# Five early attention heads by another softmax path, and the last batch's feed-forward part in two halves of its tokens

## The chip, the cores and the metric

The kernel runs on one core of one Trainium2 chip. Its time is the device time of one execution in microseconds (us), as the median of several runs of the same program. One further execution was recorded by the hardware profiler; the profile and the trace are those of that execution, and their times count from the start of its span. The engines are called TensorE (PE in the profile, with PEld for its weight loads), VectorE (DVE), ScalarE (ACT), GpSimd (POOL) and SyncE (SP, which issues most of the transfers).

## What is computed

The input `x` holds 16 batches of 512 tokens of 128 numbers. Each batch goes through one attention block and one feed-forward block (FFN), each with a layernorm in front, one behind, and a residual addition:

```
x = x + layernorm(attention(layernorm(x)))
x = x + layernorm(ffn(layernorm(x)))

attention: q, v = projections of x, 16 heads of 8 numbers
  bucket[s,h] = 6 sign bits of (q[s,h], 1) @ hyperplanes
  scores      = q q^T / sqrt(128)
  attn        = softmax(scores * (62 + [bucket equal]))       512 x 512 a head
  out         = attn @ v

ffn: h = silu(x W1^T * s1) * (x W2^T * s2)                    128 -> 512
     h = gelu(h H1^T * sh1);  h = gelu(h H2^T * sh2)          512 -> 512, twice
     y = h W3^T * s3                                          512 -> 128
```

The matrix of scores is symmetric: the queries stand in for the keys. All is float32, but for the score products, which are made of three bfloat16 parts of q, and the coefficients 62 and 63.

## The kernel before, in words

The tokens of a batch are four tiles (t = 0 to 3) of 128. There are 16 x 16 = 256 heads, numbered j through all batches, in groups of four.

**The order of the work is written by a planner.** The class `Order` (lines 47 to 187) is a small simulator that runs while the program is built. Each piece of work is a Python generator that yields steps: an engine, a planned cost in us, a rank and a function that emits the instructions. The planner keeps a clock for each engine, takes the ready step of lowest rank (ties by the order of offering), and emits it. ScalarE's choice also counts the time at which the step became ready, and 4 us for a change of activation table. `Pool` objects hold the names of buffers; `get` and `put` take and return them. On the chip each engine then runs its instructions in exactly this order, and waits where data isn't there.

**One head** takes this way:
1. `gather` (788) reads the head's q parts and bucket numbers from DRAM into `ql`, `qr`, `bb`.
2. `scores` (838): TensorE multiplies, one 128x512 tile a t, into one of three PSUM banks (`sp`).
3. `coeffs` (855): VectorE compares buckets and gives 62 or 63 (`co`, four buffers).
4. `logits` (879): VectorE multiplies the two into a logits tile `l` and writes each row's maximum to a column of `mxpad` (line 894). There are 11 buffers for `l` (`LB`); a head keeps its buffer until its group is through the av matmuls.
5. `maxima` (919): for a pair of heads (the first four heads go singly) VectorE transposes the maxima, SP writes them to DRAM (`md`, 928) and reads them back to all partitions (`mb`, 940, three buffers). Since the matrix is symmetric, the maximum of row s is also that of column s, and the weights come out turned, as the av matmul needs them.
6. `softmax` (933): GpSimd subtracts `mb` from the whole head, 128x2048 in one instruction (947); ScalarE takes the exponent in place (952).
7. `attend` (957): when four heads are done, TensorE multiplies them with v (`av`, 973; a column of ones in v gives the sums for the division), ScalarE copies, TensorE turns the result back (`op`, 994), VectorE divides.

**After the four groups of a batch** `residual` (1018) normalizes the output, adds x, normalizes again and turns the result (`tp_f`); `ffn` (1041) does the gates `w` (1088), two layers `hp` (1122), each with a ScalarE activation in pairs of 512 columns, and the last product `yp` (1156); then a last layernorm (`moments`, `rescale`), an addition (1180) and the output (1186). The FFN's matmuls have the lowest rank on TensorE; FFN b begins when FFN b-1 has finished its first hidden layer. `moments` (385) ends in a power -1/2 on GpSimd (450), of one column for each tile.

**At the start** there is little for TensorE, and `activity` (1244) fills it with matmuls of zeros until the first FFN begins. `weights` loads and scales the FFN's weights; `inputs` (510) makes the first layernorm's statistics of later batches on ScalarE.

Of the kernel before, what the change touches and what calls it, by code (L numbers as in the profile page):

```python
# [16 lines left out]
ALU = mybir.AluOpType  # L17
# [173 lines left out]
def tile_lsh_attention_ffn(  # L191
# [43 lines left out]
    LB = 11  # L235
    SLOTS = H * NT
# [130 lines left out]
    mb_bufs = Pool("mb", 3)  # L367
    h_bufs = Pool("h", 3)
# [16 lines left out]
    def moments(src, name, rank, copy=None):  # L385


        q = name[0]
        rs = p2.tile([P, NT], F32, tag=f"rs{q}", name=f"rs_{name}")
        nm = p2.tile([P, NT], F32, tag=f"nm{q}", name=f"nm_{name}")  # L390
        if copy is not None:

            sums = p2.tile([P, 2, NT], F32, tag=f"su{q}", name=f"su_{name}")
# [22 lines left out]
            yield act(1.0, -2, lambda: sum_((0, 1)))  # L416
            yield act(1.0, -2, lambda: sum_((2, 3)))
            src = copy[0]
            copy[1]()
            yield act(1.2, -2, lambda: square((0, 1)))  # L420
            od.loose()
            yield act(1.2, -2, lambda: square((2, 3)))
            mean, var = sums[:, 0, :], sums[:, 1, :]
            factor, sign = float(E) ** -3, -1.0 / E
        else:
            st = p2.tile([P, NT, nc.vector.BN_STATS_DIM], F32, tag=f"st{q}", name=f"st_{name}")
# [5 lines left out]
            def aggr():  # L432
                for t in range(NT):
                    nc.vector.bn_aggr(mv[:, t, :], st[:, t, :])

            yield dve(0.46, rank, lambda: stats((0, 1)))
            od.loose()
            yield dve(0.46, rank, lambda: stats((2, 3)))
            mv = p2.tile([P, NT, nc.vector.BN_AGGR_DIM], F32, tag=f"mv{q}", name=f"mv_{name}")
            yield dve(0.7, rank, aggr)  # L440
            mean, var, sign, factor = mv[:, :, 0], mv[:, :, 1], -1.0, 1.0
        ve = p2.tile([P, NT], F32, tag=f"ve{q}", name=f"ve_{name}")
# [4 lines left out]
                ve, var, AF.Identity, bias=eps if factor == 1.0 else eps3, scale=factor  # L447
            ),
        )
        yield pool(1.0, 0, lambda: nc.gpsimd.tensor_tensor(rs, ve, mhalf[:, 0], op=ALU.pow))  # L450

        def negate():

            for t in range(NT):
                nc.vector.tensor_scalar(
                    nm[:, t : t + 1],
                    mean[:, t : t + 1],
                    sign,
                    rs[:, t : t + 1],
                    op0=ALU.mult,  # L460
                    op1=ALU.mult,
                )

        yield dve(0.28, rank, negate)
        return nm, rs

    def rescale(src, dst, scales):

        nm, rs = scales

        def emit(ts_):
            for t in ts_:
                nc.scalar.activation(
                    dst(t),
                    src[:, t, :],
                    AF.Identity,
                    bias=nm[:, t : t + 1],
                    scale=rs[:, t : t + 1],
                )

        yield act(0.88, -2, lambda: emit((0, 1)))
        yield act(0.88, -2, lambda: emit((2, 3)))

    def turned(xn, xnt_tag, name, k, tp):


        def turn():
            for t in range(NT):
                nc.tensor.transpose(tp[:, ts(t, P)], xn[:, t, :], ident)

        yield pe(0.5, 2, turn)
        xnt = p1.tile([P, S], F32, tag=xnt_tag, name=f"xnt_{name}")
        yield act(0.5, -2, lambda: nc.scalar.copy(xnt, tp))
        od.put(banks, k)
        return xnt

    def norm_transposed(src, xnt_tag, name, rank):

        xn = p2.tile([P, NT, E], F32, tag=f"xn{name[0]}", name=f"xn_{name}", bufs=1)
        scales = yield from moments(src, name, rank)  # L500
        yield from rescale(src, lambda t: xn[:, t, :], scales)
        k = yield get(banks)
        return (yield from turned(xn, xnt_tag, name, k, bank(k, f"tp_{name}")))
# [78 lines left out]
    def prep(b):  # L582
# [14 lines left out]
        if b:  # L597
            yield wait(known[b])
            xn = p2.tile([P, NT, E], F32, tag="xna", name=f"xn_a{b}", bufs=1)
            yield from rescale(xt, lambda t: xn[:, t, :], (nm_x[:, b], rs_x[:, b]))  # L600
            k = yield get(banks)
            xnt = yield from turned(xn, "xnta", f"a{b}", k, bank(k, f"tp_a{b}"))
        else:
            xnt = yield from norm_transposed(xt, "xnta", f"a{b}", 1)
# [274 lines left out]
    def logits():  # L879
        for j in range(B * H):  # L880
            kl = yield get(logit_bufs)
            if j < SINGLES or j % MH == 0:
                km, pair = (yield get(mx_bufs)), []
                mx = mxpads[int(km[2:])]
            l = p1.tile([P, NT, S], F32, tag=kl, name=f"l_{j}")
            base = len(pair) * NT
            for t in range(NT):
# [5 lines left out]
                def emit(t=t + base, sp=sp, co=co, l=l[:, t, :], mx=mx):  # L893
# [17 lines left out]
            ls[j] = (l, kl)  # L911
            pair.append((j, l))
            if j < SINGLES or len(pair) == MH:
                od.spawn(maxima(pair, mx, km))
# [39 lines left out]

    o_tiles = {}

    def attend(gg):
# [24 lines left out]
        for k in range(GH):  # L982
            od.put(logit_bufs, ls.pop(gg * GH + k)[1])
# [34 lines left out]
    def residual(b):  # L1018
# [10 lines left out]
        scales = yield from moments(o, f"o{b}", 1)  # L1029
        kb = yield get(banks)  # L1030
        ybt = bank(kb, f"yb_{b}").rearrange("p (t e) -> p t e", t=NT)
        yield from rescale(o, lambda t: ybt[:, t, :], scales)
        k1 = yield get(x1_bufs)
        x1 = p1.tile([P, NT, E], F32, tag=k1, name=f"x1_{b}")
        yield dve(0.6, 1, lambda: nc.vector.tensor_tensor(x1, ybt, xt, op=ALU.add))
        od.put(banks, kb)
        kx = yield get(xnt_bufs)
        xnt = yield from norm_transposed(x1, kx, f"f{b}", 1)
        od.spawn(ffn(b, x1, k1, xnt, kx))

    def ffn(b, x1, k1, xnt, kx):
# [4 lines left out]
        kh = yield get(h_bufs)  # L1046
        h = p1.tile([P, NC, S], F32, tag=kh, name=f"h_{b}_0")
        there = events(NC)

        def product(w2, c, half, held, h=h, there=there):  # L1050
            yield wait(half)
            kb, g2 = w2
            a, ka = held[c % 2]
            yield dve(
                0.66,
                1,
                lambda: nc.vector.tensor_tensor(h[:, c, :], g2, a, op=ALU.mult),  # L1057
            )
            od.put(ffn_banks, kb)
# [3 lines left out]
        def silus(c0, gates, half, held):  # L1063
            for _ in gates:
                held.append((yield get(a_bufs)))
            tiles = [
                p1.tile([P, S], F32, tag=ka, name=f"a_{b}_{c0 + i}")
# [3 lines left out]
            def emit():  # L1071
                for i, (a, (_, gp)) in enumerate(zip(tiles, gates)):
# [3 lines left out]
            yield act(1.2, 0, emit, "silu")  # L1076
            for kb, _ in gates:
                od.put(ffn_banks, kb)
            held[:] = zip(tiles, list(held))
            od.set(half)  # L1080

        def gate(which, c):
            kb = yield get(ffn_banks)
            gp = bank(kb, f"{which}_{b}_{c}")
            yield pe(
                0.86,
                4,
                lambda: nc.tensor.matmul(  # L1088
                    gp, lhsT=w_sb[which][:, 0, ts(c, P)], rhs=xnt, start=True, stop=True
                ),  # L1090
            )
            return kb, gp

        for c0 in range(0, NC, 2):
            gates = []
            for c in (c0, c0 + 1):
                gates.append((yield from gate("w1", c)))
            half, held = Event(), []
            od.spawn(silus(c0, gates, half, held))
            for c in (c0, c0 + 1):  # L1100
                w2 = yield from gate("w2", c)
                od.spawn(product(w2, c, half, held))
        od.put(xnt_bufs, kx)
        od.set(stages[b][0])

        for layer in (1, 2):
            w = w_sb[f"h{layer}"]
            hin, khin, before = h, kh, there
            kh = yield get(h_bufs)
            h = p1.tile([P, NC, S], F32, tag=kh, name=f"h_{b}_{layer}")  # L1110
            there = events(NC)
            for c0 in range(0, NC, 2):
                got = []
                for c in (c0, c0 + 1):
                    kb = yield get(ffn_banks)
                    hp = bank(kb, f"hp_{b}_{layer}_{c}")
                    for i in range(NC):
                        yield wait(before[i])
                        yield pe(
                            0.86,  # L1120
# [4 lines left out]
                                rhs=hin[:, i, :],  # L1125
# [4 lines left out]
                    got.append((c, kb, hp))  # L1130

                def gelus(got=got, h=h, there=there, sc=w_sb[f"h{layer}s"]):
                    def emit():
                        for c, _, hp in got:
                            nc.scalar.activation(  # L1135
                                h[:, c, :], hp, AF.Gelu, scale=sc[:, c : c + 1]
                            )

                    yield act(1.2, 0, emit, "gelu")
                    for c, kb, _ in got:  # L1140
                        od.put(ffn_banks, kb)
                        od.set(there[c])

                od.spawn(gelus())
            od.put(h_bufs, khin)
            od.set(stages[b][layer])
# [4 lines left out]
        yp = bank(kb, f"yp_{b}")  # L1151
        for t in range(NT):
# [12 lines left out]
        od.put(h_bufs, kh)  # L1165
        od.set(stages[b][3])


        y = p2.tile([P, NT, E], F32, tag="y", name=f"y_{b}", bufs=1)
# [3 lines left out]
            1,  # L1173
            (y, lambda: od.put(ffn_banks, kb)),
        )
        kn = yield get(banks)
        ybt = bank(kn, f"yn_{b}").rearrange("p (t e) -> p t e", t=NT)
        yield from rescale(y, lambda t: ybt[:, t, :], scales)
        z = y
        yield dve(0.6, 1, lambda: nc.vector.tensor_tensor(z, ybt, x1, op=ALU.add))  # L1180
        od.put(banks, kn)
        od.put(x1_bufs, k1)
# [3 lines left out]
            lambda: nc.sync.dma_start(out=out[b].rearrange("(p t) e -> p t e", t=NT), in_=z),  # L1186
# [134 lines left out]
```

## Time and profile before

| what | value |
|---|---|
| median of 3 runs | 1375.74 us (1370.01 to 1375.81) |
| the profiled execution | 1373.08 us |
| its span in the trace | 1371.3 us |
| mean granted TensorE clock | 0.991 |
| busy: PE, DVE, ACT, POOL | 1317.3, 1236.0, 1127.8, 1217.1 us |
| GpSimd's subtractions (947) | 256 of 4552 ns, 1156.1 us |
| logits (894) | 1024 of 681 ns; a new one can start every 0.60 us |
| coefficients (865) | 1024 of 472 ns; one every 0.39 us |
| exponents (952) | 256 of 1907 ns |
| FFN matmuls of 512 columns (1122, 1088) | one each 0.43 us |
| activation tables loaded before lines 952 and 1135 | 86 and 58, of 1283 ns |

How to read it: a row of the profile names the line, the engine, the operation, the tiles (out<-in), how often it ran, and its mean duration. Instructions of one engine overlap a little, so the distance from one start to the next can be shorter than a duration. The durations of matmuls are modelled; the distance from start to start is the safer figure. The 40 digits of an engine are tenths of busy time in 40 equal slices of the span. The granted clock is TensorE's, 1.00 at full speed. "Idle before" tells how long an engine waited ahead of an instruction, and for whom.

### The profile page before, as it was taken

To read this page: it belongs to the slowest core of one execution; us is meant where nothing else is said; L and a number is where in the kernel's file an instruction comes from. 1 tells how busy PE (TensorE), PEld (TensorE's weight loads), DVE (VectorE), ACT (ScalarE), POOL (GpSimd) and SP (SyncE) were. 2 spreads that over 40 slices of the span, in tenths; PEclk is the share of its full clock that TensorE was granted. 3 is DMA by queue.
4 is the path that set the end of the run, shared out by engine and by line. 5 is a ranking of instruction groups with operands and counts; after the bars stand their busy time and mean duration, and the time that the engine had idled before them with its cause. 6 is when DMAs were issued, how large, how long until landed. Compare 5 with 4: busy or idle time off the path is not lost.

```text
span 1371.3 us, 21177 instructions
## 1 busy us (share of the span) xinstructions
PE 1317.3 (96%) x5922; PEld 550.9 (40%) x5922; DVE 1236.0 (90%) x3989; ACT 1127.8 (82%) x1607; POOL 1217.1 (89%) x319
## 2 busy tenths in 40 slices
PE   9999999999889999999999999999999999999996
PEld 3433334334334434343434434343434434343443
DVE  5999999999889999999999999999999999998210
ACT  2567798999779888988989888988989888988852
POOL 1599999999999999999999999999999999999400
PEclk9999999999899999999999999999999999999998
DMA  5756455445435455445545455454545454453000
GB/s 143 194 148 157 133 150 145 140 140 141 134 106 153 125 130 142 138 138 132 147 116 147 129 134 135 139 139 135 142 124 141 135 134 135 132 122 101 24 8 8
DMA packets 159837, 175.39 MB, mean 128 GB/s; under 512 B 34280, under 2 KB 117480, under 8 KB 159720
## 3 DMA queue, kind: packets, MB, share of 16 engines
q1 hardware_dynamic: 156909, 170.56, 45.4%
q10 hardware_dynamic: 2811, 3.48, 0.8%
q8 instruction: 47, 0.77, 0.2%
q14 instruction: 70, 0.57, 0.1%
HBM read 154.81 MB, written 19.17 MB: 127 GB/s over the span
## 4 chain that ended last, share of the span: by engine, by line
PE 50%; DVE 24%; POOL 9%; issue 8%; DMA 6%; ACT 2%; SPq 1%; POOLq 0%; DVEq 0%; ACTq 0%
PE hp L1122 18%; PE av L973 12%; DVE l L894 11%; PE sp L847 9%; DVE co L865 8%; POOL l L947 8%; PE w L1088 4%; PE yp L1156 3%; DMA mb<-md 3%; DMA bb<-bkd 1%; DMA qd<-q 1%; PE op L994 1%; PE vp L760 1%; POOL rs_x L561 1%; DMA qr<-qd 1%
## 5 line engine op out<-in xcount | busy, mean ns | idle before, releaser
L947 POOL TENSOR_TENSOR l<-l,mb 128x2048 f32<-128x2048 f32 x256 | 1156.1, 4552 | 43.4 <-DVE mxpad L894 24.0
L894 DVE CUSTOM_DVE_ANT_0 l<-co,sp 128x512 f32<-128x512 bf16 x1024 | 665.7, 681 | 13.8 <-PE av L973 6.9
L952 ACT ACTIVATE l<-l 128x2048 f32<-128x2048 f32 x256 | 484.6, 1907 | 40.9 <-POOL l L947 39.4
L1122 PE MATMUL hp<-h,h 128*128 128x512 f32 x1024 | 498.6, 596 | 0.3 <-ACT h L1135 0.3
L865 DVE TENSOR_SCALAR co<-bb,bj 128x516 bf16<-128x516 bf16 x1024 | 455.0, 472 | 3.3 <-DMA bb<-bkd 3.1
L847 PE MATMUL sp<-qr,ql 72*128 72x512 bf16 x1024 | 358.0, 382 | 26.7 <-DVE mxpad L894 22.5
L1122 PEld LDWEIGHTS hp<-h,h 128*128 128x128 f32 x1024 | 190.1, 190 | 185.6 <-issue 151.6
L973 PE MATMUL av<-l,vaug 128*32 128x512 f32 x2048 | 263.6, 603 | 0.0
L847 PEld LDWEIGHTS <-ql 72*128 72x128 bf16 x1024 | 94.1, 97 | 313.9 <-issue 290.7
L1088 PE MATMUL w<-xnt_f,w 128*128 128x512 f32 x256 | 132.0, 601 | 2.5 <-ACT a L1074 2.4
L952 ACT ACT_TABLE_LOAD x86 | 110.3, 1283 | 1.5
L1251 PE MATMUL activity<-still 128*128 128x512 bf16 x402 | 106.6, 385 | 1.0 <-DVE still L280 1.0
L973 PEld LDWEIGHTS av<-l,vaug 128*32 128x32 f32 x2048 | 47.4, 109 | 116.5 <-issue 93.9
L894 DVE DVE_READ_ACCUMULATOR2_ANT mxpad<- 128x1 f32 x1024 | 85.7, 84 | 0.0
L450 POOL TENSOR_TENSOR rs_y<-ve_y,mhalf 128x4 f32<-128x4 f32 x16 | 16.1, 1006 | 67.1 <-issue 34.7
L1057 DVE TENSOR_TENSOR h<-w,a 128x512 f32<-128x512 f32 x64 | 43.7, 682 | 35.2 <-PE w L1088 30.3
L1135 ACT ACT_TABLE_LOAD x58 | 74.4, 1283 | 0.9
L987 ACT COPY avs<-av 128x512 f32<-128x512 f32 x64 | 37.0, 578 | 40.0 <-PE av L973 39.9
L1088 PEld LDWEIGHTS w<-xnt_f,w 128*128 128x128 f32 x256 | 46.9, 191 | 53.1 <-issue 21.8
L1156 PEld LDWEIGHTS yp<-w,h 128*128 128x128 f32 x512 | 65.0, 196 | 7.3 <-issue 4.0
L1156 PE MATMUL yp<-w,h 128*128 128x128 f32 x512 | 66.6, 281 | 0.1
L1251 PEld LDWEIGHTS <-still 128*128 128x128 bf16 x402 | 39.1, 99 | 56.5 <-issue 19.0
(94 smaller groups left out, 941.7 us busy)
## 6 DMA issues: line engine op xcount, KB each, us to landing
mb<-md SPq DMA_DIRECT2D x256, 256.0 KB
bb<-bkd SPq DMA_DIRECT2D x256, 130.5 KB
ql<-qd SPq DMA_DIRECT2D x256, 72.0 KB
qr<-qd SPq DMA_DIRECT2D x255, 72.0 KB
qd<-q SPq DMA_DIRECT2D x96, 128.0 KB
xta<-in_L_attn_x_dram SPq DMA_DIRECT2D x16, 256.0 KB
xtr<-in_L_attn_x_dram SPq DMA_DIRECT2D x16, 256.0 KB
out_dram<-y SPq DMA_DIRECT2D x16, 256.0 KB
```

Source lines behind the costliest of these rows:

```text
L847: nc.tensor.matmul(sp, lhsT=ql[:, ts(t, P)], rhs=qr, start=True, stop=True)
L865: nc.vector.tensor_scalar(co, bb.rearrange("p (r c) -> p r c", c=BP)[:, :, 0:BC], bjs[b][:, c : c + 1], float(NBKT - 2), op0=ALU.is_equal, ...
L894: nc.vector.tensor_tensor_reduce(out=l, in0=co[:, 0:S], in1=sp, scale=1.0, scalar=-3.0e38, op0=ALU.mult, op1=ALU.max, accum_out=mx[:, t : ...
L947: lambda: nc.gpsimd.tensor_tensor(l, l, mb.unsqueeze(1).to_broadcast([P, NT, S]), op=ALU.subtract),
L952: yield act(1.82, 0, lambda: nc.scalar.activation(l, l, AF.Exp, scale=SCALE), "exp")
L973: nc.tensor.matmul(av[k * Q : (k + 1) * Q, :], lhsT=va[:, t, c : c + Q], rhs=ls[gg * GH + k][0][:, t, :], start=(t == 0), stop=(t == NT - 1),)
L1057: lambda: nc.vector.tensor_tensor(h[:, c, :], g2, a, op=ALU.mult),
L1088: lambda: nc.tensor.matmul(gp, lhsT=w_sb[which][:, 0, ts(c, P)], rhs=xnt, start=True, stop=True),
L1122: lambda i=i: nc.tensor.matmul(hp, lhsT=w[:, i, ts(c, P)], rhs=hin[:, i, :], start=(i == 0), stop=(i == NC - 1),),
L1135: nc.scalar.activation(h[:, c, :], hp, AF.Gelu, scale=sc[:, c : c + 1])
L1156: nc.tensor.matmul(yp[:, ts(t, E)], lhsT=h[:, i, ts(t, P)], rhs=w_sb["w3"][:, i, :], start=(i == 0), stop=(i == NC - 1),)
L1251: nc.tensor.matmul(bk, lhsT=still, rhs=still.unsqueeze(1).to_broadcast([P, NT, P]), start=start, stop=stop,)
```

## The change

It has two parts.

**By rows.** For heads 3, 7, 11, 15 and 19 the maxima don't travel through DRAM, and GpSimd doesn't subtract. The four maxima of each partition stay where they are, in a tile `mx` of their own; ScalarE scales them to a bias, takes the exponents in four instructions of 128x512 with that bias for each row; TensorE turns the 16 squares of 128x128 into PSUM, a bank for each column tile; and ScalarE copies the four banks into `w`, a tile from the FFN's three `h` buffers. The av matmuls then read `w` in place of `l`. The other heads form pairs as they come, so that 6 pairs with 8, and 14 with 16.

**Two halves.** For the last batch alone `residual` starts two pieces, tiles 0 and 1, and tiles 2 and 3. Each half goes through its own layernorms, its own FFN with matmuls of 256 columns, and its own output. The two halves share the tiles `x1`, `xnt`, `h` and `y`. In a half, two results of 256 columns share one PSUM bank. All other batches do what they did, by the same instructions.

The core of the diff:

```diff
+    BY_ROWS = (3, 7, 11, 15, 19)
...
+    row_mx_bufs = Pool("rx", 2)
...
     def logits():
+        pair = []
         for j in range(B * H):
             kl = yield get(logit_bufs)
-            if j < SINGLES or j % MH == 0:
-                km, pair = (yield get(mx_bufs)), []
-                mx = mxpads[int(km[2:])]
+            by_rows = j in BY_ROWS
+            if by_rows:
+                kr = yield get(row_mx_bufs)
+                mx_, base = p1.tile([P, NT], F32, tag=kr, name=f"mx_{j}"), 0
+            else:
+                if not pair:
+                    km = yield get(mx_bufs)
+                    mx = mxpads[int(km[2:])]
+                mx_, base = mx, len(pair) * NT
...
+            if by_rows:
+                od.spawn(softmax_by_rows(j, l, kl, mx_, kr))
+            else:
+                pair.append((j, l))
+                if j < SINGLES or len(pair) == MH or j == B * H - 1:
+                    od.spawn(maxima(pair, mx, km))
+                    pair = []
...
+    def softmax_by_rows(j, l, kl, mx, kr):
+        nmx = p1.tile([P, NT], F32, tag="n" + kr, name=f"nmx_{j}")
+        yield act(0.22, -5, lambda: nc.scalar.activation(nmx, mx, AF.Copy, scale=-SCALE))
+
+        def weigh():
+            for t in range(NT):
+                nc.scalar.activation(
+                    l[:, t, :], l[:, t, :], AF.Exp, bias=nmx[:, t : t + 1], scale=SCALE
+                )
+
+        yield act(2.3, 0, weigh, "exp")
+        od.put(row_mx_bufs, kr)
+        kh = yield get(h_bufs)
+        w = p1.tile([P, NT, S], F32, tag=kh, name=f"w_{j}")
+        there = events(NT)
+
+        def evict(t, tp, k):
+            yield act(0.5, -2, lambda: nc.scalar.copy(w[:, t, :], tp))
+            od.put(banks, k)
+            od.set(there[t])
+
+        for t in range(NT):
+            k = yield get(banks)
+            tp = bank(k, f"tw_{j}_{t}")
+
+            def turn(t=t, tp=tp):
+                for i in range(NT):
+                    nc.tensor.transpose(tp[:, ts(i, P)], l[:, i, ts(t, P)], ident)
+
+            yield pe(0.45, 1, turn)
+            od.spawn(evict(t, tp, k))
+        od.put(logit_bufs, kl)
+        for e in there:
+            yield wait(e)
+        ls[j] = w, h_bufs, kh
+        od.set(exped[j])
...
+        parts = (ALL,) if b < B - 1 else HALVES
+        hs = []
+        for tiles in parts:
+            od.spawn(added(b, tiles, o, xt, x1, k1, xnt, kx, hs))
...
+    def ffn(b, tiles, x1, k1, xnt, kx, hs):
+        whole = tiles == ALL
+        n = len(tiles) * P
+        cols = slice(tiles[0] * P, tiles[0] * P + n)
+        cost = 0.86 * n / S
...
+        def two_banks(name):
+
+            k0 = yield get(ffn_banks)
+            b0 = bank(k0, f"{name}_{b}_{tiles[0]}_0")
+            if not whole:
+                return [b0[:, 0:n], b0[:, n : 2 * n]], [k0]
+            k1_ = yield get(ffn_banks)
+            return [b0, bank(k1_, f"{name}_{b}_{tiles[0]}_1")], [k0, k1_]
```

`moments`, `rescale` and `turned` take the list of tiles to work on, and the power, the scaling and the copy then cover that many columns.

## The prediction

> **What bounds the kernel now.** I read the page first, then the table of busy time by stretches, then the waits of GpSimd and of VectorE, then the timelines of both around single heads, and the chain and timeline of the end. On the page three engines look full:
>
> ```profile
> DVE  5999999999889999999999999999999999998210
> ...
> POOL 1599999999999999999999999999999999999400
> PEclk9999999999899999999999999999999999999998
> ```
>
> Of a core with several full engines the one that never waits sets the pace. The table by stretches (time, then busy us of PE, PEld, DVE, ACT, POOL, then the granted clock) shows which one that is, and where:
>
> ```profile
> 68.00:150.00 82.00, 80.79 (x429) 29.86 (x428) 78.39 (x247) 58.60 (x115) 82.00 (x20) 1.00 0.55 150
> 150.00:300.00 150.00, 143.71 (x664) 58.34 (x666) 146.11 (x470) 134.67 (x211) 149.28 (x38) 1.00 0.50 143
> 300.00:400.00 100.00, 88.30 (x384) 36.07 (x375) 92.00 (x304) 86.39 (x139) 94.45 (x24) 0.95 0.49 133
> 400.00:1240.00 840.00, 822.59 (x3747) 343.54 (x3747) 832.26 (x2683) 740.19 (x927) 821.18 (x209) 1.00 0.49 134
> ...
> 1300.00:1362.00 62.00, 60.55 (x190) 30.40 (x188) 6.36 (x22) 24.74 (x60) 2.01 (x2) 1.00 0.01 4
> ```
>
> From 68 to 150 us GpSimd is the one without a gap. From 400 to 1240 it is VectorE: 832.3 of 840 us, 7.7 us idle, against 18.8 on GpSimd. From 1300 on it is TensorE alone. GpSimd's own waits from 400 to 1240 are mostly for the tiny power of a layernorm, not for heads; and VectorE's waits from 28 to 150 us are led by logits that wait for a free buffer, which the av matmul gives back:
>
> ```profile
> POOL rs_o L450 <- ACT ve_o L446: 11.1, 5, 3.0
> ...
> POOL l L947 <- DMA mb<-md: 1.8, 2, 1.2
> ```
>
> ```profile
> DVE l L894 <- PE av L973: 2.4, 3, 1.2
> ```
>
> How far GpSimd lies behind VectorE is read off the timelines, from the end of a head's fourth logits tile to the start of its subtraction. Head 20: 122.6 to 143.8, 21.2 us. Head 52: 278.8 to 292.7, 13.9 us. Head 252: 1250.8 to 1263.4, 12.6 us. A head cannot follow sooner than its maxima travel: it waits for its pair (about 4 us), then the transpose, the write to DRAM and the read back (head 52: transpose at 283.7, read issued 288.7, subtraction 292.7), some 10 us at the least. So GpSimd has a backlog of about 10 us only until head 50; after that it follows VectorE as closely as it can. VectorE's last logits end at 1263.2; between head 20 and there it needs 1140.6 us for 235 heads, 4.85 us each. GpSimd would need 4.53 plus three powers a batch, 3 x 1.0 / 16: 4.72. VectorE is the slower one.
>
> **Part 1, five heads by rows.** Removed from GpSimd: 5 x 4.55 = 22.8 us (heads 3, 7, 11, 15, 19 begin at 63 to 138 us); with them five reads of 256 KB and their issues (0.4 us each) from SP's queue. Pairs are now formed of what is left, so 127 maxima trips stand where 130 stood: 3 transposes of 0.2 us less on VectorE, 0.6 us. The logits themselves stay: 20 tensor_tensor_reduce and 20 coefficients for the five heads are untouched.
>
> Does VectorE get faster when GpSimd is quieter? The rows say no. Logits while GpSimd was idle (27 to 40 us) and while it was full (1000 to 1100 us):
>
> ```profile
> L894 DVE CUSTOM_DVE_ANT_0 l<-co,sp 128x512 f32<-128x512 bf16 x13 | 8.4, 684 | 0.0
> ```
>
> ```profile
> L894 DVE CUSTOM_DVE_ANT_0 l<-co,sp 128x512 f32<-128x512 bf16 x83 | 54.2, 681 | 0.7 <-PE sp L847 0.5
> ```
>
> So the 22.8 us count only where GpSimd was the pace, and that is before head 50. There VectorE idled 3.6 us from 68 to 150 and 3.9 us from 150 to 300. I count the 3.6 (buffers come back sooner), 1.0 of the 3.9 (the backlog was still there in its first third), and the 0.6: 5.2 us. The bounds: nothing, if those waits return at scores or at DMA, and 0.6 + 1.4 + 3.6 + 3.9 = 9.5 us, if VectorE ran from 28 to 300 without a gap. The rest of the 22.8 turns into GpSimd waiting for VectorE's maxima.
>
> Added on ScalarE, per head: one scaling of the maxima (0.2 to 0.3, as ve), four exps of 128x512 with a bias per row (nearest row: q <- qp with a bias, 0.68, a new one every 0.57; so 2.3, against 1.9 for the one exp removed), four evictions (0.56 each as xnt_a, 2.2). That is about +3 us a head, 15 us in all. ScalarE was busy 17.6 of 40 us from 28 to 68 and 58.6 of 82 from 68 to 150, so 46 us were free: counted at nothing. Without this cover the exps of the next heads would come up to 15 us late.
>
> Added on TensorE: 16 transposes a head; four take 0.44 (op L994), so 1.8 us a head and 8.8 in all, in place of the idle matmuls of `activity` (402 of them, one each 0.216 us), which run until the first FFN begins. Cost nothing on the path, but they add a wait: the transposes stand in TensorE's queue until the head's exps are done, and behind them stand the scores, for which VectorE waits. ScalarE once stood 7.0 us before an x tile (60 to 67 us), just when head 7's exps fall due (its logits end at 62.9). Three score banks and four coefficient buffers cover about 3 x 0.6 + 4 x 0.39 = 3.4 us. Bounds: 0, and 5 x 2 us if every one of the five comes late by some 5 us. The av matmuls already wait for exps in the same way, and VectorE lost 0.2 us at scores from 68 to 150: I take 0. Below nothing it can't be.
>
> **Part 2, the last batch in halves.** After the last matmul (1360.7) the end is a chain in which each step works on four tiles; the halves leave two behind the last matmul:
>
> ```profile
> 1364.26 1.01 POOL L450 TENSOR_TENSOR rs_y<-ve_y,mhalf 128x4 f32<-128x4 f32 x1 [34.67 <-issue]
> ...
> 1365.55 1.95 ACT L473 ACTIVATE yn<-y,nm_y,rs_y 128x128 f32<-128x128 f32 x4 [1.42 <-DVE nm_y L455]
> 1367.52 0.69 DVE L1180 TENSOR_TENSOR y<-yn,x 128x512 f32<-128x512 f32 x1 [1.65 <-ACT yn L473]
> ```
>
> Sums 1360.69 to 1361.71, half is 0.51. Squares to 1363.83, half is 1.06. The power: 4 columns take 1.00, 16 take 2.93 and 40 take 6.76, so 0.16 a column, 0.32 saved. Rescaling 1.95, half is 0.98. The addition 0.69 goes to about 0.42 (128x128 from the same memory is 0.29, L1005): 0.27. Output 256 KB ends 3.1 us after the addition; half of it saves 0 to 0.5, I take 0.2. Together 3.3 us. Against it: the first half's own rescaling and output share ScalarE with the second half's sums (0 to 1.0, taken 0.5), and the FFN's matmuls become twice as many with 256 columns.
>
> Here a rule of the Trainium skill speaks against the change. *TensorE: Matmul & The Clock Gate*, section *Why this matters for your kernels*, advises for matmuls under 512 columns to pad or to keep the loop together, since otherwise the clock falls back to half. By that rule 160 matmuls more at half clock would cost up to the whole 34 us of this FFN again. The row nearest to it is yp: 32 matmuls of 128 columns, each with weights of its own, in 3.76 us at a granted clock of 1.00, that is 0.1175 each where a quarter of 0.43 is 0.1075. They follow one another without gaps, so neither clock nor weight loading costs more than 0.01 each. By the trace 160 x 0.0045 (the spacing inside yp is 0.112) = 0.7 us; at most 1.6. I take 0.7. Both halves are offered with the same rank, so their matmuls alternate and both end close together. At a change of layers each waits for its gelus; with two streams one covers the other. Part 2: 3.3 - 0.5 - 0.7 = 2.1 us; bounds -3 (a silu and a gelu table of 1.28 each loaded in turn on the path, twice) and +4. The half-sized residual starts FFN 15 earlier, but TensorE is full with FFN 14 then: nothing.
>
> **The sum.** The profiled execution took 1373.08 us (span 1371.3 and 1.8 around it): 1373.08 - 5.2 - 2.1 = 1365.8. The median of the runs is 2.66 above it; on that scale 1375.74 - 7.3 = **1368.4**.
>
> **The rivals.** *Everything moves with GpSimd* (15%). For it: from 68 to 300 us it has gaps of 0.7 us in all, and batch 0's output (133.9) comes 35 us after its logits, so FFN 0, which starts at 169.9, could start some 13 to 18 us sooner and replace idle matmuls. If that lead were kept to the end, 18 + 2 = 20 us: 1355.7. Against it: an FFN starts 36 us (batch 0) to 40 us (batch 14) after its own attention, not after a backlog, and attention is paced by VectorE.
>
> *The clock falls* (22%, slower). TensorE halves its clock once it has stood nearly idle for some us:
>
> ```profile
> 330.00:340.00 10.00, 6.82 (x31) 2.40 (x33) 10.00 (x33) 9.94 (x22) 10.00 (x4) 1.00 0.58 156
> ...
> 350.00:360.00 10.00, 5.81 (x15) 1.52 (x14) 9.72 (x26) 8.36 (x16) 10.00 (x4) 0.68 0.63 172
> 360.00:370.00 10.00, 10.00 (x49) 2.99 (x47) 6.46 (x19) 7.40 (x8) 8.11 (x2) 0.81 0.40 121
> ```
>
> Those 20 us cost VectorE 3.8 us, and the stretch 300 to 400 8.0. The page named above, section *What's actually happening*, says the same of one idle window of about 3.4 us. Now `activity` ends sooner and FFN 0 and 1 are through sooner, while FFN 2 still waits for its attention (290.8): the hole before it widens by up to 13 us. Two further dips of 8 us each bring 1375.74 - 7.3 + 16 = 1384. It decides from the point at which TensorE's holes before 400 us hold two more windows than now.
>
> *No change* (18%): the 5.2 us return at scores behind the transposes, and the halves eat their 2.1: 1375.7. That the five subtractions stay on GpSimd cannot be: the code has no other path for them.
>
> **How the numbers follow.** Forecast 45%, own range 1360 to 1374; GpSimd 15%; clock 22%; no change 18%. Half a percent is 6.9 us, about what a measurement of this kernel can tell from no change. Faster by more: all of the second case and 0.29 of the first, 0.44. Slower by more: the clock case, 0.22. Within: 0.34. The range reaches from 1353 to 1386.
>
> **What would show it.** Right: subtractions 251 instead of 256; GpSimd with gaps from head 20 on and 10 to 14 us behind VectorE at once; the last logits within 1255 to 1263; TensorE's end some 5 us earlier; last matmul to end about 8 us instead of 10.6. Wrong: the last logits before 1250 (the lead was kept), VectorE waiting for scores in the first 150 us, clock under 1.00 in more stretches than 350 to 370, or hp matmuls of 256 columns above 0.225 us each.

## The result, and the profile after

The changed kernel takes 1369.04 us in the median of 15 runs (1366.31 to 1371.57), the kernel before 1374.0 beside it: a ratio of 0.9965, 95% interval [0.9955, 0.9976], or 4.8 us less. The forecast was 1368.4, 7.3 us less. The profiled execution after took 1371.57 us, the longest of its 15, with a span of 1369.8. That is 1.5 us less than the profiled execution before, so the two traces show the route of the change better than its size.

The page after, with the three engines that looked full, TensorE's granted clock and the group of the subtractions:

```profile
DVE  4999999799998999999999999999999999999220
POOL 1398989999899998999989999998999999899810
PEclk9999999899999999999999999999999999999999
...
L991 POOL TENSOR_TENSOR l<-l,mb 128x2048 f32<-128x2048 f32 x251 | 1135.6, 4566 | 56.8 <-DMA mb<-md 41.5
```

There are 251 subtractions, and the idle time before them is 56.8 us where it was 43.4. Between 28 and 150 us most of it is for maxima that are still on their way; the 20.7 stand ahead of the first subtraction, where the kernel before waits 21.2 us too:

```profile
POOL l L991 <- DMA mb<-md: 26.0, 4, 20.7
```

From 68 to 150 us, where GpSimd had no gap, it is now idle for 8.4 of 82 us (the first row below). The distance from a head's last logits to its subtraction fell from 21.2 to 12.5 us at head 20, and from 19.0 to 14.7 on average over heads 20 to 49; from head 60 on it is 16.0, and was 14.8. What became of VectorE is in the busy times of the same stretches as before (time, then PE, PEld, DVE, ACT, POOL, then the clock):

```profile
68.00:150.00 82.00, 81.66 (x469) 35.94 (x469) 81.78 (x268) 67.84 (x148) 73.62 (x19) 1.00 0.50 143
150.00:300.00 150.00, 141.80 (x609) 56.71 (x608) 141.57 (x450) 132.78 (x211) 139.28 (x35) 0.95 0.49 139
300.00:400.00 100.00, 96.16 (x425) 39.92 (x425) 97.47 (x319) 89.59 (x147) 93.10 (x24) 0.98 0.46 131
400.00:1240.00 840.00, 817.30 (x3693) 339.83 (x3693) 820.09 (x2642) 733.75 (x919) 811.92 (x206) 1.00 0.48 134
...
1300.00:1362.00 62.00, 61.03 (x298) 45.26 (x296) 9.25 (x41) 28.17 (x76) 3.74 (x5) 1.00 0.01 5
```

VectorE's idle time, before and after: 28 to 150 us, 5.0 and 2.7; 150 to 300, 3.9 and 8.4; 300 to 400, 8.0 and 2.5; 400 to 1240, 7.7 and 19.9. Together 8.9 us more, and its last logits end at 1271.2 where they ended at 1263.2. In the long stretch its longest waits were for scores; now they are for other results of TensorE. First before, then after:

```profile
DVE l L894 <- PE sp L847: 3.1, 13, 0.3
```

```profile
DVE rd L1087 <- PE op L1077: 8.7, 12, 1.4
DVE l L934 <- PE av L1056: 5.5, 4, 3.2
DVE h L1178 <- PE w L1208: 2.2, 4, 1.3
```

These 8.0 us come back behind the last logits. FFNs run closer behind their attention: from the last `op` of a batch to its FFN's layernorm power (`rs_y`) it is 135 us instead of 161 (mean of batches 4 to 12). So less FFN is left over when attention ends: counted in matmuls of 512 columns, 156 gates and hidden products instead of 171, which at 0.43 us are 6.5 us. TensorE's end lies 90.8 us behind the last logits instead of 97.5, at 1362.0 (before 1360.7), and from there to the end it is 7.8 us instead of 10.6. The span's change is 8.0 - 6.7 - 2.8 = -1.5 us.

### The profile page after: what moved, and what is told of

Its sections match the earlier page's. It is cut to its first block, busy times and chain, and to the rows that moved or that the text cites. A ratio compares the mean times of both kernels' runs of the same rounds, so it can differ in the third digit from the quotient of the medians.

```text
span 1369.8 us, 21290 instructions
## 1 busy us (share of the span) xinstructions
PE 1316.2 (96%) x6008; PEld 568.3 (41%) x6008; DVE 1234.5 (90%) x3992; ACT 1143.8 (84%) x1665; POOL 1197.4 (87%) x317
## 4 chain that ended last, share of the span: by engine, by line
PE 57%; DVE 24%; POOL 6%; issue 6%; DMA 4%; ACT 3%; SPq 0%; ACTq 0%; POOLq 0%; DVEq 0%
PE hp L1252 25%; PE av L1056 13%; DVE l L934 12%; PE sp L881 10%; DVE co L899 8%; POOL l L991 6%; PE w L1208 3%; DMA mb<-md 2%; PE yp L1290 2%; PE op L1077 2%; DMA bb<-bkd 1%; ACT l L996 1%; PE vp L794 1%; PE activity L1396 1%; DVE h L1178 1%
## 5 line engine op out<-in xcount | busy, mean ns | idle before, releaser
L991 POOL TENSOR_TENSOR l<-l,mb 128x2048 f32<-128x2048 f32 x251 | 1135.6, 4566 | 56.8 <-DMA mb<-md 41.5
L996 ACT ACTIVATE l<-l 128x2048 f32<-128x2048 f32 x251 | 477.8, 1907 | 23.3 <-POOL l L991 22.1
L1252 PE MATMUL hp<-h,h 128*128 128x512 f32 (+1 forms) x1088 | 494.3, 570 | 0.1
L1252 PEld LDWEIGHTS hp<-h,h 128*128 128x128 f32 x1088 | 201.4, 190 | 160.3 <-issue 137.7
L1208 PE MATMUL w<-xnt_f,w 128*128 128x512 f32 (+1 forms) x272 | 133.1, 585 | 4.3 <-ACT a L1196 2.6
L1396 PE MATMUL activity<-still 128*128 128x512 bf16 x328 | 88.8, 387 | 1.0 <-DVE still L281 1.0
L1208 PEld LDWEIGHTS w<-xnt_f,w 128*128 128x128 f32 x272 | 50.9, 195 | 51.1 <-issue 20.8
L1178 DVE TENSOR_TENSOR h<-w,a 128x512 f32<-128x512 f32 (+1 forms) x68 | 44.2, 656 | 29.4 <-PE w L1208 18.9
L1290 PEld LDWEIGHTS yp<-w,h 128*128 128x128 f32 x512 | 65.7, 193 | 11.3 <-issue 6.7
L469 POOL TENSOR_TENSOR rs_y<-ve_y,mhalf 128x4 f32<-128x4 f32 (+1 forms) x17 | 16.7, 985 | 48.4 <-ACT ve_y L458 47.8
L1266 ACT ACTIVATE h<-hp,h1s 128x512 f32<-128x512 f32 (+1 forms) x68 | 41.8, 660 | 14.9 <-PE hp L1252 14.5
```

The lines of the kernel that those rows point to most:

```text
L991: lambda: nc.gpsimd.tensor_tensor(l, l, mb.unsqueeze(1).to_broadcast([P, NT, S]), op=ALU.subtract),
L996: yield act(1.82, 0, lambda: nc.scalar.activation(l, l, AF.Exp, scale=SCALE), "exp")
L1178: lambda: nc.vector.tensor_tensor(h[:, c, cols], g2, a, op=ALU.mult),
L1208: lambda: nc.tensor.matmul(gp, lhsT=w_sb[which][:, 0, ts(c, P)], rhs=xnt[:, cols], start=True, stop=True),
L1252: lambda i=i: nc.tensor.matmul(hp, lhsT=w[:, i, ts(c, P)], rhs=hin[:, i, cols], start=(i == 0), stop=(i == NC - 1),),
L1266: nc.scalar.activation(h[:, c, cols], hp, AF.Gelu, scale=sc[:, c : c + 1])
```

## The experiments

Each was timed against the kernel before. "Period" is the time of 16 heads, averaged from head 80 to 224 at their last logits (before 77.32 us); "distance" is that from `op` to `rs_y`; "half speed" is the time at a halved clock in the trace's clock record, without what lies behind the last matmul (before 17.1 us).

**Each part alone, in the changed code.** First the halves, then the rows:

```diff
-    BY_ROWS = (3, 7, 11, 15, 19)
+    BY_ROWS = ()
```

> The changed kernel with no heads by rows: only the last batch's two halves are left. Theory (the end after the last matmul is all that the change gains): last matmul to end 7.8 us instead of 10.6, TensorE's end within 1.5 us of the kernel before, so 2 to 3.5 us faster than before, ratio 0.9975 to 0.9985. Rival (the heads by rows bring the larger part, through the earlier first FFN): 0 to 2 us faster.

```diff
-        parts = (ALL,) if b < B - 1 else HALVES
+        parts = (ALL,)
```

> The changed kernel with the last batch whole, as before: only the five heads by rows are left. Theory (VectorE and TensorE pace the middle; GpSimd's lead is lost): 0 to 2.5 us faster than before, last logits later than before by up to 8 us and the FFNs closer behind their attention. Rival (the earlier start is kept): 10 to 18 us faster. Rival (the transposes in TensorE's queue hold VectorE up): slower than before, with VectorE waiting for scores in the first 150 us. The two parts' gains should add up to the 4.8 us of the whole.

Halves only: ratio 1.024 [1.0219, 1.026], 33 us slower, which no theory had. Its end after the last matmul is 7.7 us, as it should be; the loss lies in the middle, where batches without any halves take 79.38 us and the distance is 183 us. So the diff holds something beside its two parts. Rows only: 1.0019 [1.001, 1.0029], 2.6 us slower. Its logits of head 80 end at 412.3 (before 416.0), its period is 78.20 and its distance 135. Up to 1308 us its trace has the same instructions in the same order as the changed kernel's, on all four engines; yet there the logits of head 80 end at 417.6 and the last logits at 1271.2 instead of 1267.7. Two single traces of one order can lie 5 us apart at a head, and the 8.0 us above have to be read with that.

**What the coupling of the engines is worth.** About 20 us of repeated work for heads 100 to 149, in a fixed order of all else: a second coefficient operation, a small second addition on GpSimd, or second score matmuls. All repeat or follow the same work and leave it otherwise alone (the addition on GpSimd works on the maxima after their use). The cuts are from the three kernels, in this order.

```diff
+                def emit(c=t * H + h, bb=bb, co=co, b=b, n=2 if 100 <= j < 150 and t == 0 else 1):
+                    for _ in range(n):
...
+            if 100 <= j < 150:
+                nc.gpsimd.tensor_tensor(
+                    mb[:, 0:160], mb[:, 0:160], mb[:, 0:160], op=ALU.add
+                )
...
+                def emit(t=t, sp=sp, ql=ql, qr=qr, n=2 if 100 <= j < 150 and t % 2 == 0 else 1):
+                    for _ in range(n):
```

> The kernel before, with the first coefficient tile of heads 100 to 149 computed twice: 50 more instructions of 0.39 us on VectorE, 19.5 us in all, in the same written-out order. Theory (VectorE paces the middle): 15 to 20 us slower. Rival (GpSimd paces it): 0 to 5 us. Rival (TensorE's total work sets the end): 0 to 5 us, with the later logits made good at the end.

> The kernel before, with one more addition of 128x160 on GpSimd behind the subtraction of heads 100 to 149: 50 x about 0.4 us, about 20 us in all, in the same written-out order. Theory (VectorE paces the middle, GpSimd has 0.13 us a head to spare): 50 x (0.4 - 0.13), 10 to 15 us slower inside these heads at first, and partly made good later: 3 to 12 us. Rival (GpSimd paces it throughout): the whole 18 to 22 us.

> The kernel before, with two of the four score matmuls of heads 100 to 149 done twice into the same bank: 100 more matmuls of 0.216 us on TensorE, 21.6 us in all, in the same written order. VectorE's 19.5 us more cost 25 us and GpSimd's 22.6 us cost 19. If all three engines are tied together by the written order, 12 to 25 us slower; if TensorE has slack there (its pitches leave some 5 us a batch, 16 us in these heads), 2 to 8 us slower.

VectorE, 19.5 us put in: 1.0186 [1.0161, 1.0212], 25.5 us. GpSimd, 22.6 us: 1.0138 [1.0117, 1.016], 19 us. TensorE, 21.6 us: 1.0132 [1.0112, 1.0152], 18 us. In the traces the delay of the logits grows within the loaded heads, by 23.4 us on VectorE, 17.3 on GpSimd and 14.6 on TensorE, and stays to the end. So no engine paces alone: the order is fixed, and of an addition on any of the three two thirds or more are paid, by the traces as by the medians.

**Each part without what else the diff moves.** Besides the parts, the diff takes two kinds of buffers earlier in every batch: `x1` and `xnt`, in `residual` ahead of the first layernorm; and both banks of the two `w1` gates ahead of the first matmul. The order of instructions is planned from when buffers are free, so much of the order changes: place by place, a third of TensorE's matmuls belong to other tiles in the changed places than in the old ones when both parts are in, and half when only the halves are. The next kernels hold for whole batches the old code at both places, and the planned cost of the power, 1.00 us, which the diff made 1.01. With the halves alone the traces then show the order of before up to 1299 us.

```diff
-            gates, kbs = yield from two_banks(f"w1_{c0}")
+            if whole:
+                gates, kbs = [], []
+            else:
+                gates, kbs = yield from two_banks(f"w1_{c0}")
...
+                if whole:
+                    kb = yield get(ffn_banks)
+                    kbs.append(kb)
+                    gates.append(bank(kb, f"w1_{b}_{c0 + i}"))
```

> The kernel before with the last batch in halves and nothing else: the buffers x1 and xnt of batches 0 to 14 are taken where they were taken before, their gates take one bank at a time, and so the written order is that of before up to the last batch. Theory (the halves gain the end after the last matmul; what made the halves alone 33 us slower is the earlier taking of buffers and banks in all batches): 2 to 4 us faster than before, ratio 0.997 to 0.9985. Rival (256-column matmuls or tables of the halves are what costs): more than 10 us slower.

> The kernel before with the five heads by rows and nothing else: buffers and banks of the FFN are taken where they were taken before. Theory of the prediction (early waits of VectorE vanish, the rest of GpSimd's lead is lost): 0 to 6 us faster. Rival (the earlier start of the first FFN is kept to the end): 10 to 18 us faster. Rival (the heads by rows only help by making up for the earlier taking of buffers): no change or slower, like the 2.6 us slower of the rows with the buffers taken early.

> The changed kernel with the buffers x1 and xnt and the banks of the gates taken where the kernel before took them, in batches 0 to 14. If the two parts are independent of one another, its gain is the sum of the gains of the two single parts in the same order, 3 to 8 us; if the earlier taking of buffers is a cost that the changed kernel pays, it is faster than the changed kernel (ratio to before under 0.9965); if it happens to be of use there, slower.

Halves: 0.9984 [0.997, 0.9998], 2.2 us less, with a period of 77.13. Rows: 1.0074 [1.0054, 1.0094], 10 us slower; period 79.50, distance 132. Both: 1.003 [1.0017, 1.0043], 4.1 slower; period 79.20. So the halves alone are worth what the forecast said, and 6 us on top of the rows; the two gains do not add. And the rows lose in this order, though heads to 80 gain (410.4 against 416.0). Nor does it pay to move the buffers back: the changed kernel is the faster one.

**The two moved buffers, each alone** (neither part of the change in them): `x1` and `xnt` early, and the two banks at once.

> The kernel before with one edit: residual takes x1 and xnt before the first layernorm of the attention's output instead of where they are written; no heads by rows, no halves. Theory (this early taking is what made the halves alone slow: the layernorm waits until the FFN before is through its gates): 20 to 35 us slower, from the attention's output to its layernorm 20 us and more instead of 4 to 9. Rival (the gates that take two banks at once are the cause): within 5 us of before.

> The kernel before with one edit: the two w1 gates take both PSUM banks before the first matmul instead of one at a time; no heads by rows, no halves, x1 and xnt taken where they were. With the early taking of xnt this made 33 us (halves alone, new order), of which the halves gain 2 and the early xnt alone costs 4. If the costs add up: 25 to 33 us slower. If each is harmless alone and only both together hold up the residual: within 8 us of before.

Buffers early: 1.0032 [1.0021, 1.0044], 4.4 us, where 20 to 35 were expected; the layernorm does wait as foreseen, 19.3 us from the last `op` to `rs_o` instead of 5.4 (batches 4 to 12). Two banks: 1.0239 [1.0221, 1.0258], 33 us, as much as the halves-only kernel lost. GpSimd's timeline shows where; first before, then with two banks:

```profile
1073.74 1.01 POOL L450 TENSOR_TENSOR rs_o<-ve_o,mhalf 128x4 f32<-128x4 f32 x1 [2.69 <-ACT ve_o L446]
...
1098.24 1.00 POOL L450 TENSOR_TENSOR rs_f<-ve_f,mhalf 128x4 f32<-128x4 f32 x1
```

```profile
1092.19 1.00 POOL L469 TENSOR_TENSOR rs_o<-ve_o,mhalf 128x4 f32<-128x4 f32 x1
...
1130.49 1.01 POOL L469 TENSOR_TENSOR rs_y<-ve_y,mhalf 128x4 f32<-128x4 f32 x1 [1.20 <-ACT ve_y L458]
...
1154.03 1.00 POOL L469 TENSOR_TENSOR rs_f<-ve_f,mhalf 128x4 f32<-128x4 f32 x1
```

`rs_o` opens a batch's residual and `rs_f` stands before its FFN. Before, 24.5 us lie between them; here 61.8, with the end of an older FFN (`rs_y`) between. This is the widest gap; over batches 4 to 12 the mean is 22.5 and 32.1. Residuals are planned behind FFNs, FFNs start late, and at the end TensorE works 114.8 us beyond the last logits (before 97.5). In the halves-only kernel, where both buffers and banks are moved, the delay stands ahead of `rs_o`: 35.9 us from the last `op` instead of 5.4. On VectorE, ScalarE and GpSimd no kind of instruction that runs 50 times or more became 2% longer.

**When the first or third FFN begins.** Both parts in the old order, with one pause written into the plan:

```diff
+        if b == 0:
+            yield ("rest", 12.0)
```

> Both parts in the old places of buffers and banks (as in e7), with one line more: the first batch's FFN is held back 12 us in the written order before its first gate, so that idle matmuls go on until then. Theory (the heads by rows save VectorE about 5 us in the first 80 heads, and e6 and e7 lose it again because their interleaving of FFN and attention makes each later batch 1 to 2 us longer): another interleaving keeps the 5 us, period of a batch under 78.3 us instead of 79.2, last logits before 1268, 6 to 12 us faster than before. Rival (an earlier first FFN is what gains): slower than the changed kernel, ratio above 0.9965. Rival (the clock's dips, 51 us in e7, are the loss): no better than e7 unless the dips go.

```diff
+        if b == 2:
+            yield ("rest", 30.0)
```

> Both parts in the old places, with the FFN of batch 2 held back 30 us in the written order, so that from there on the FFNs run as far behind their attention as in the kernel before (about 160 us from a batch's attention to its last layernorm, against 132 in e6 and e7). Theory (the interleaving with the short distance is what makes batches longer): period back to 77.2 to 77.8 us, last logits 1258 to 1264, TensorE's end some 97 us behind them, 2 to 7 us faster than before. Rival (the five heads by rows themselves cost the 10 us of e6, by transposes and banks): as slow as e7.

First held: 0.9964 [0.995, 0.9977], 5 us faster than before and 9 better than the same kernel without the pause. Its first gate starts at 166.7 us instead of 152.9, and yet TensorE ends 4.5 us sooner (1363.6, 1368.1). Distance (132) and period (78.90 against 79.20, both profiled) stay nearly as they were, and half speed in the trace falls from 51.2 to 27.3 us. The theory's own marks were missed (a period under 78.3, last logits before 1268; they end at 1275.4); what came is the condition of the rival of the clock's dips. Third held: 0.9996 [0.9985, 1.0006], no change against before, where 2 to 7 us less were expected; the distance of 166, the period of 77.54 and the last logits at 1264.5 came close to what the theory had; half speed 30.7. VectorE waits again as little as before; the first of these lines is the rows in the old order, the second the third FFN held:

```profile
400.00:1240.00 840.00, 816.61 (x3666) 339.18 (x3665) 814.21 (x2619) 726.02 (x914) 803.88 (x203) 0.99 0.48 133
```

```profile
400.00:1240.00 840.00, 822.09 (x3742) 342.62 (x3741) 830.27 (x2677) 740.52 (x926) 817.40 (x207) 1.00 0.50 135
```

No kernel that was run is clearly better than the changed one; the first FFN held equals it within both intervals.

**The clock over all timed executions.** Within the kernel before, the 29, 23 and 17 executions of three series get longer by 0.83, 1.02 and 0.92 us for each 0.001 that the mean granted clock is lower (correlation -0.8 to -0.9): in the second from 1371.3 us at 0.993 to 1378.3 at 0.986. By 0.9 us the differences split so (the clock's share is an estimate from that rate, the rest is what remains; the series of the changed kernel recorded no clock of the kernel before, and 0.991 is taken):

| kernel | against before, us | mean clock (before 0.991 to 0.992) | share of the clock | rest | period, us | half speed in heads 80 to 224, us |
|---|---|---|---|---|---|---|
| changed | -4.8 | 0.990 | +1.3 | -6.1 | 78.01 | 3.4 |
| both, old order | +4.1 | 0.981 | +9.0 | -4.9 | 79.20 | 20.5 |
| both, first FFN held | -5 | 0.991 | +0.3 | -5.3 | 78.90 | 10.2 |
| both, third FFN held | -0.5 | 0.987 | +3.5 | -4.0 | 77.54 | 3.4 |
| rows only, changed code | +2.6 | 0.989 | +3.0 | -0.4 | 78.20 | 6.8 |
| rows, old order | +10 | 0.980 | +9.9 | +0.1 | 79.50 | 23.9 |
| halves, old order | -2.2 | 0.991 | 0 | -2.2 | 77.13 | 0 |

The four kernels with both parts lie 9 us apart as measured and 2 us apart at one clock. By the same rate 9 of the 33 us of the two banks would be the clock's. Period and half speed go up together. That is a relation and no proof of direction: a stretch in which TensorE has nothing to do may both cost time by itself and bring the clock down.

## Why the prediction was right, and where it was not

The time was met (1369.04 us against 1368.4), and in good part by luck: neither term of the sum came as forecast in this kernel. The rows were to bring 5.2 us and the halves 2.1. In the changed code the rows alone are 2.6 us slower than before, and the halves on top of them bring 7.4 (by the ratios of two series); in the old places it is 10 slower and 6. Two errors of opposite sign cancel. The gain itself, 4.8 us with an interval of 3.3 to 6.2, is less than the forecast's 7.3; the times agree better than the gains because the kernel before has a median of 1374.0 in its 15 runs and had 1375.74 in the three that the forecast started from.

*Bound.* "VectorE is the slower one", with slack on GpSimd, was the wrong picture. VectorE had the least idle time, but 22.6 us added to GpSimd cost 19 and 21.6 us on TensorE cost 18 (17 and 15 in the traces). Least idle told who waits least, not that the others have room.

*Part 1, the early gain (5.2 us).* The first term was right: VectorE's 3.6 us of waits from 68 to 150 us became 0.2, though from 28 to 68 it idles about 1 more. In the two kernels with the rows alone the logits of head 80 end 3.7 and 5.6 us sooner than before, about the size of the forecast. The second term, 1.0 from 150 to 300, had the wrong sign: 4.5 more. The step that failed is that later batches keep what the early heads gain: they take 78.2 and 79.5 us instead of 77.3, and the last logits of the two kernels end 4.5 and 16.7 us later. Slices of 10 us show where the first loss lies; the changed kernel:

```profile
230.00:240.00 10.00, 6.64 (x22) 3.06 (x22) 10.00 (x36) 9.00 (x26) 10.00 (x3) 0.80 0.37 108
240.00:250.00 10.00, 10.00 (x46) 2.99 (x45) 6.73 (x21) 9.91 (x13) 10.00 (x4) 0.86 0.46 140
250.00:260.00 10.00, 7.21 (x23) 3.08 (x22) 9.97 (x31) 7.35 (x13) 10.00 (x3) 0.82 0.33 107
260.00:270.00 10.00, 10.00 (x23) 3.69 (x21) 9.35 (x26) 9.17 (x11) 10.00 (x3) 0.84 0.45 138
```

From 230 to 240 TensorE stands for 3.4 us, its clock falls, and from 240 to 250 it is full at 0.86 while VectorE idles 3.3 us. Before, the clock is 1.00 in all four slices. This is the hole of the rival *the clock falls*, one FFN earlier: FFN 0 starts at 154.2 instead of 169.9 and ends at 230.8, while FFN 1 waits for its attention until 237.9; before, FFN 0 ended at 253.3, after FFN 1 had begun at 246.1. A second hole follows at 253 to 258, in the middle of FFN 1's gates. All six kernels profiled with the rows have half speed between 230 and 243 us; none without them has. Between 300 and 400 the old dip at 354 (10.2 us of half speed) shrank to 3.4, and 5.5 us came back. So the rival's condition, two more windows of half speed before 400 us, was met (20.5 us instead of 10.2), but the timed executions give the clock only about 1.3 us. In the old order it is 9 to 10 us against the rival's "16" for two further dips of 8.

*"The rest of the 22.8 turns into GpSimd waiting"*, and 10 to 14 us behind: right for heads 20 to 27 (11.3 to 13.1 us); heads 28 to 49 are 12.5 to 17.3 behind, and later ones 16.0 on average, more than the 14.8 of the kernel before.

*The transposes at no cost*, and ScalarE's 15 us: right for the first 150 us, where VectorE waits 0.4 us for scores and TensorE had idle matmuls to give (402 became 328).

*What the prediction did not have* is a cost of the step that the description of the change gives as "All other batches do what they did". The same instructions run, in another order. It was counted at nothing, while one of the two moved buffers costs 33 us by itself and the other 4.4; with the rows in place, the changed order ended better than the old (0.9965 against 1.003). Their sizes do not add, so this was luck and not judgement. The "last logits 1255 to 1263" failed: 1271.2. The moved buffers are not the reason, for in the old places the logits end later still (1277.6 with both parts): with the rows the planner interleaves FFNs and attention differently in all batches, wherever the buffers are taken. That TensorE would end 5 us earlier failed in the profiled pair (1.3 later). The sum came near because TensorE ends 6.7 us sooner behind the last logits, a term that the prediction did not contain: 3.0 of it come with the rows alone (94.5 us instead of 97.5), by FFNs closer behind attention, and 3.7 with the halves on top (90.8).

*Everything moves with GpSimd* fell: a first FFN 14 us later ended TensorE 4.5 us earlier. FFN work done early was not a lead that was kept.

*Part 2 (2.1 us)* was right in mechanism and size where all else is as before: 2.2 in the old order. From the last logits to the end the traces give 108.1 us before and 106.0 with the halves; the part after the last matmul went from 10.6 to 7.8 us, the forecast's 3.3 - 0.5, and the part ahead of it grew by 0.7, the forecast's third term. (Its "160 matmuls more" are 80 more: 160 of 256 columns stand for 80 of 512.) On top of the rows the halves bring more: 105.4 to 98.6 us in the changed code, 103.2 to 98.3 in the old places. About 3 us of each lie after the last matmul as before; 3.7 and 2.1 lie ahead of it. There "TensorE is full with FFN 14 then: nothing" did not hold: with less FFN left over, TensorE pauses at the gates of the last FFN. First the rows alone, then the changed kernel, whose halves run between one another and FFN 14's last product:

```profile
1321.40 2.84 PE L1208 MATMUL w<-xnt_f,w 128*128 128x512 f32 x6 [0.76 <-ACT xnt_f L515]
1325.88 2.41 PE L1208 MATMUL w<-xnt_f,w 128*128 128x512 f32 x5 [1.65 <-ACT a L1196]
```

```profile
1325.90 4.58 PE L1208 MATMUL w<-xnt_f,w 128*128 128x256 f32 x20 [0.92 <-DVE h L1178]
```

In the changed code a half-speed stretch of 3.4 us in the trace of the rows alone, which the other trace lacks, may be up to 1.7 of the 3.7 us. The last steps of the timeline after:

```profile
1364.21 0.70 POOL L469 TENSOR_TENSOR rs_y<-ve_y,mhalf 128x2 f32<-128x2 f32 x1 [0.54 <-POOL rs_y L469]
...
1365.54 0.95 ACT L495 ACTIVATE yn<-y,nm_y,rs_y 128x128 f32<-128x128 f32 x2 [0.61 <-DVE nm_y L477]
1366.52 0.42 DVE L1321 TENSOR_TENSOR y<-yn,x 128x256 f32<-128x256 f32 x1 [0.90 <-ACT yn L495]
```

0.70, 0.95 and 0.42 stand where 1.01, 1.95 and 0.69 stood. And the chain of its matmuls:

```profile
1330.53 27.89 PE hp L1252 x128
1358.43 3.58 PE yp L1290 x32
```

128 matmuls of 256 columns in 27.89 us are 0.218 each, under the 0.225 set as the limit (half of 0.43 is 0.215), at a clock of 1.00. The rule that the forecast set against this, in the Trainium skill, *TensorE: Matmul & The Clock Gate*, section *Why this matters for your kernels*, asks for thin products either to be padded or to have their loop kept together; this stream is kept together, and the trace agrees with the rule. What went with a lower clock here was a hole in TensorE's work, as at 230 us.

*What stays open.* By the medians the halves bring 7.4 and 6 us on top of the rows, and by the traces 6.8 and 4.9 at the end; the rest, about 1 us, is within the noise. Why the planner's order with the rows makes later batches longer was not followed to a single step. And whether the clock costs the time or only marks the holes was not separated: a kernel with holes and a full clock was not tried.

## What to carry to other kernels

Where a planner writes the order, an edit of when a buffer is taken is a change of every batch, though no instruction is added; run it by itself before counting it at nothing. An engine's idle time does not say what added work costs: put in a known load and see how much of it comes out. Measure a part alone and on top of the other parts: here one part is worth 2 us alone and 6 to 7 with the other. Work that is brought forward is only worth something if the engine that gets it has no hole behind it, and the granted clock can tell whether one opened.

## What the runs showed of the hardware

Mean clock and time of one unchanged kernel move together from execution to execution: 0.986 to 0.993, and 1378.3 to 1371.3 us. Half-speed stretches in the traces, up to the last matmul, came as 3.4, 6.8 or 10.2 us. The power of two columns on GpSimd took 0.70 us, of four 1.01: 0.37 + 0.16 a column gives 0.69 and 1.01.
